# A long-convolution and routed low-rank FFN kernel: the tables' last steps behind the gates, row sums and gate transposes on the Vector engine

## The chip, the cores and the metric

The kernel runs on one core of a Trainium2 chip. The metric is the time of one execution in device microseconds (us); lower is better. The core has five engines that each work through their own instructions in order: TensorE (PE, matrix products), VectorE (DVE), ScalarE (ACT), GpSimd (POOL) and SyncE (SP). DMA transfers are started from the queues of SP, ACT and POOL. [...]

## The reference

The input x has shape (64 batches, 64 heads, 1024 positions). For every head h a convolution kernel K of length 1024 is made from 64 complex modes, and each row is convolved with it and masked by a length per batch. The result goes through a layer of 64 low-rank experts, of which each token uses 16, and x is added.

```
dtA = A * dt[:, None]                                  # 64 heads x 64 modes, complex
Cs  = Cc * (exp(dtA) - 1) / A
K   = 2 * real(einsum('hn,hnl->hl', Cs, exp(dtA[:, :, None] * arange(1024))))
y   = causal_conv(x * mask, K) + x * mask * D[:, None]; y = y * mask

scores = y @ Wr.T                                      # 4096 tokens x 64 experts
top_vals, top_idx = top_k(scores, 16); gates = softmax(top_vals)
G   = zeros.at[token, top_idx].set(gates)
h   = einsum('nd,krd->nkr', y, A)                      # 64 experts of rank 16: 1024 columns
out = einsum('nkr,kdr->nd', h * G[:, :, None], B)
return x + 2 * out
```

## The kernel before, in words

The 4096 tokens are 64 heads times 64 batches. They are worked through in eight groups g of eight heads, 512 tokens each. A group has these stages:

- **Tables** (`tables(g)`, lines 237 to 347, a generator whose yields let other work come in between). Vector and Scalar make the powers of the modes: f, k and a clamp on Vector, Sin and Exp on Scalar, and from them w (real and imaginary part, 129 positions). From w come the tiles b (`L320` on Scalar, `L366` on Vector), which PE transposes against the identity (pb, `L326`); Scalar copies them to bt (`L330`). The first 128 values of K of each head are the sums of b over the modes. PE takes these sums as a product with a tile of ones (pk, `L293`, a result of 2 partitions by 512); Scalar copies it to ks, Vector adds D to the first column, and SP writes the rows to memory (krows) and reads them back as Toeplitz tiles (toep).
- **Convolution** (`conv(g)`, line 595). PE forms the states of seven blocks (pu, `L620`), Scalar copies them to s, and Vector runs a recurrence over the blocks (`recur`, `L366`, three instructions per block and pair of heads; four pairs a group). PE adds the part inside a block (pc from x and toep, `L649`) and that of earlier blocks (pc from s and w, `L658`), and Vector applies the mask and writes y (`L666`).
- **Gates** (`gates(g)`, line 722). PE computes scores (psh, `L728`, eight products into two halves of a bank), Scalar copies them to sh, and PE transposes sh (psc, `L737`) so that tokens lie on partitions. Vector adds the two halves (sc), takes the 16 largest by two rounds of max and match_replace, and with Scalar's Exp forms the softmax in the tile sa.
- **Spreading the gates** (`spread_gates`, line 768). PE transposes sa back (pg, `L772`), Scalar copies pg to gt, and a DMA on Scalar's queue writes gt to memory. Eight DMAs (on GpSimd's queue, for the last group on SP's) read it back as gx, each gate repeated for the 16 ranks of its expert.
- **First product** (`first`, line 795). h = y times A, by a seven-product scheme on quarters (`seven`, `L553`, products 1, 6, 2, 7, 5, 4, 3 for each of two column blocks j). Vector and GpSimd combine the products (u, p), multiply them by the gates gx into the tile hg, and form sums of hg; GpSimd's queue stores hg to memory.

While a group's convolution is computed, the products of the group before fill PE. After all groups, a second stage (`second`, from about 630 us on) computes h times B in two levels of the same scheme.

The order of instructions on each engine comes from a scheduler that works at build time from the order of the program and the dependences; some rows are pinned with `tc.keep_in_program_order`. Buffers count: the PSUM pool ps_k (two banks) serves pb, pk, pu, psh, psc and pg; ps_f (four banks) serves h; the tables' tiles mag, f, k and sn are single, and k and sn are reused as the tiles b. The tile gt is reused for sh.

The last yields of `tables(g)` are taken here, at the end of `conv` of the group before:

```
last_two = inside(2), inside(3)
across(*last_two[0])
across(*last_two[1])
step(6)                       # the last steps of the next group's tables
```

The main loop then calls `gates(g, y)`, runs what is left of the tables' steps, starts the products of the group, and calls `spread_gates`.

Of the kernel before, what the change touches and what calls it, by code (L numbers as in the profile page):

```python
# [37 lines left out]
F32 = mybir.dt.float32  # L38
I32 = mybir.dt.int32
AF = mybir.ActivationFunctionType  # L40
ALU = mybir.AluOpType
AX = mybir.AxisListType
PSUM = bass.MemoryType.PSUM

P = 128
# [5 lines left out]
NE = 64  # L51
# [3 lines left out]
HG = 8  # L55
NG = NH // HG
TOK = HG * NB
NTT = TOK // P
# [5 lines left out]
GP = HG // 2  # L64
NW = P + 1
NCH = NBLK - 1
KROW = P - 1 + P
# [22 lines left out]
    return c  # L90


def body(ctx: ExitStack, tc, x, xo, lens, par, dvec, at, bm, wt, cst, out):
    nc = tc.nc
    V = nc.vector
    G = nc.gpsimd
# [11 lines left out]
    ps_k = psum.enter_context(tc.tile_pool(name="ps_k", bufs=2, space=PSUM))  # L108
# [4 lines left out]
    gp = pool(left, "gp", 1, "left")  # L113
    tq = pool(left, "tq", 1, "left")
    ids = pool(ctx, "ids", 1, "right")
    const = pool(right, "const", 1, "right")
    xp = pool(right, "xp", 4, "right")
    tp = pool(right, "tp", 1, "right")
    tabp = pool(right, "tabp", 1, "right")
# [8 lines left out]
    cst_sb = ids.tile([P, NW + P + 2 + NBLK], F32, tag="cst", name="cst_sb")  # L128
    nc.scalar.dma_start(cst_sb, cst)
    lens_sb = prep.tile([P, NB], I32, tag="lens", name="lens_sb")  # L130
    d_sb = const.tile([2, NP], F32, tag="dvec", name="d_sb")
    nc.scalar.dma_start(d_sb, dvec)
    lv = cst_sb[:, :NW]
    ident = cst_sb[:, NW : NW + P]
    heads = cst_sb[:, NW + P : NW + P + 2]
# [2 lines left out]
    krows = dram.tile([NH, KROW], F32, tag="krows", name="krows")  # L138
# [98 lines left out]
    def tables(g):  # L237

        j0 = g * GP
        wide = [P, GP, NW]

        def new(t, name=None):
            return tabp.tile(wide, F32, tag=t, name=f"{name or t}_{g}")

        mag, f, k = new("mag"), new("f"), new("k")
        for i in range(GP):
            nc.scalar.activation(mag[:, i, :], lv, AF.Exp, scale=dt_re[:, j0 + i : j0 + i + 1])
        tt(f, tu_hi[:, j0 : j0 + GP].unsqueeze(2).to_broadcast(wide),  # L250
           lv.unsqueeze(1).to_broadcast(wide), ALU.mult)
        yield
        ts(k, f, MAGIC, ALU.add, MAGIC, ALU.subtract)
        yield
        tt(f, f, k, ALU.subtract)
        yield
        for i in range(GP):
            stt(f[:, i, :], lv, tu_lo[:, j0 + i : j0 + i + 1], ALU.mult, f[:, i, :], ALU.add)
            if i % 2:
                yield  # L260
        ts(f, f, HALF_IN, ALU.min, -HALF_IN, ALU.max)

        sh, sn = new("k", "sh"), new("sn")
        nc.scalar.activation(sh, f, AF.Sin, scale=math.pi)
        nc.scalar.activation(sn, f, AF.Sin, scale=2.0 * math.pi)
        nc.scalar.activation(sh, sh, AF.Square)
        nc.scalar.activation(sh, sh, AF.Copy, scale=-2.0, bias=1.0)
        yield
        w = tab2.tile([P, 2, GP, NW], F32, tag="w", name=f"w_{g}")
        tt(w[:, 1], mag, sn, ALU.mult)  # L270
        yield
        tt(w[:, 0], mag, sh, ALU.mult)
        yield
        alpha, nbeta, nalpha = (scales[q] for q in ("alpha", "nbeta", "nalpha"))
        bt = tp.tile([P, GP, 2 * P], F32, tag="bt", name=f"bt_{g}")

        def others():
            return (tab2.tile([P, 3, GP], F32, tag="turn", name=f"turn_{g}"),
                    tp.tile([P, HG, P], F32, tag="toep", name=f"toep_{g}"))

        if g == 0:
            turn, toep = others()
            tabs[g] = (w, bt, turn, toep)
        h0 = g * HG
        all_rows = tabp.tile([2, GP, P], F32, tag="ks", name=f"ks_{g}")

        def kernels(bbs, i):


            n = i + 2 * len(bbs)  # L290
            pk = ps_k.tile([2, n - i, P], F32, tag="pk", name=f"pk_{g}_{i}")
            for m, bb in enumerate(bbs):
                nc.tensor.matmul(pk[:, 2 * m : 2 * m + 2, :], lhsT=heads, rhs=bb[:, :, 0, :],  # L293
                                 start=True, stop=True)
            ks = all_rows[:, i:n, :]
            nc.scalar.copy(ks, pk)
            return ks, i, n

        def rows(ks, i, n):

            tt(ks[:, :, 0], ks[:, :, 0], d_sb[:, j0 + i : j0 + n], ALU.add)
            row = krows[h0 + 2 * i : h0 + 2 * i + 1, :]
            nc.sync.dma_start(
                krows[h0 + 2 * i : h0 + 2 * n, P - 1 :].rearrange("(i a) l -> a i l", a=2), ks)
            nc.sync.dma_start(toep[:, 2 * i : 2 * n, :],
                              bass.AP(row.tensor, row.offset, [[1, P], [KROW, 2 * (n - i)], [1, P]]))

        bbs, halves = [], []
        for i in range(GP):
            j = j0 + i  # L310
            re, im = w[:, 0, i, :P], w[:, 1, i, :P]
            if i % 2 == 0:
                bb = tabp.tile([P, 2, 2, P], F32, tag=("sn", "k")[i // 2], name=f"b_{g}_{i}")
                bbs.append(bb)
            b = bb[:, i % 2]
            for c, by in enumerate((alpha, nbeta)):
                if g == 0:
                    ts(b[:, c, :], re, by[:, j : j + 1], ALU.mult)
                else:
                    nc.scalar.activation(b[:, c, :], re, AF.Copy, scale=by[:, j : j + 1])  # L320
            stt(b[:, 0, :], im, nbeta[:, j : j + 1], ALU.mult, b[:, 0, :], ALU.add)
            stt(b[:, 1, :], im, nalpha[:, j : j + 1], ALU.mult, b[:, 1, :], ALU.add)
            if g == 0 or i % 2 == 0:
                pb = ps_k.tile([P, 1 if g == 0 else 2, 2 * P], F32, tag="pk", name=f"pb_{g}_{i}")
            for c in range(2):
                nc.tensor.transpose(pb[:, i % 2 if g else 0, (1 - c) * P : (2 - c) * P], b[:, c, :], ident)  # L326
            if g == 0:
                nc.scalar.copy(bt[:, i, :], pb[:, 0])
            elif i % 2:
                nc.scalar.copy(bt[:, i - 1 : i + 1, :], pb)  # L330
            if g == 0 and i % 2:
                halves.append(kernels(bbs[i // 2 :], i - 1))
            if g == 0 and i == 3:
                rows(*halves[0])
            yield
        if g:
            turn, toep = others()
        V.tensor_copy(turn[:, 0:2], w[:, :, :, P])
        ts(turn[:, 2], turn[:, 1], -1.0, ALU.mult)
        if g == 0:  # L340
            yield
            rows(*halves[1])
            return
        ks = kernels(bbs, 0)
        yield
        rows(*ks)
        tabs[g] = (w, bt, turn, toep)


# [4 lines left out]
    def tt(o, a, b, o_):  # L354
        V.tensor_tensor(out=o, in0=a, in1=b, op=o_)  # L355
        return o
# [54 lines left out]
    s, q = parts  # L411
# [183 lines left out]
    def conv(g, steps, out):  # L595
        if g == 0:
            next(steps)
        w, bt, turn, toep = tabs.pop(g)
# [74 lines left out]
        def step(n):  # L673
            for _ in range(n):
                next(steps, None)
# [40 lines left out]
        last_two = inside(2), inside(3)  # L716
        across(*last_two[0])
        across(*last_two[1])
        step(6)


    def gates(g, y):
        yf = y.rearrange("p k s h b -> p k (s h b)")

        phalf = ps_k.tile([P, TOK], F32, tag="pk", name=f"psh_{g}")
# [4 lines left out]
                start=(d < 2), stop=(d >= NBLK - 2),  # L730
            )
        sh = gp.tile([P, TOK], F32, tag="gt", name=f"sh_{g}")
        nc.scalar.copy(sh, phalf)

        pscore = ps_k.tile([P, NTT, 2, NE], F32, tag="pk", name=f"psc_{g}")
        for t in range(NTT):
# [13 lines left out]
        for t in range(NTT):  # L750
# [3 lines left out]
        ex = sa  # L754
# [8 lines left out]
            out=ex, in0=ex, in1=rd.unsqueeze(2).to_broadcast([P, NTT, NE]), op=ALU.mult)  # L763
        return ex

    gt_dram = dram.tile([NG, NE, TOK], F32, tag="gt", name="gt_dram")

    def spread_gates(g, ex, spread):

        pg = ps_k.tile([NE, TOK], F32, tag="pk", name=f"pg_{g}")  # L770
        for t in range(NTT):
            tc.keep_in_program_order(nc.tensor.transpose(pg[:, t * P : (t + 1) * P], ex[:, t, :], ident))  # L772
        gt = gp.tile([NE, TOK], F32, tag="gt", name=f"gt_{g}")
        nc.scalar.copy(gt, pg)
        nc.scalar.dma_start(gt_dram[g], gt)
        n = P // RANK
        queue = nc.sync if g + 1 == NG else G
        for j in range(0, KH, 2):
            for m in range(2):
                gx = gxp.tile([P, 2, TOK], F32, tag="gx", name=f"gx_{g}_{j}_{m}")  # L780
                for ii in range(2):
                    c = m * KH + j + ii
                    i = queue.dma_start(  # L783
                        gx[:, ii, :],
                        gt_dram[g, c * n : (c + 1) * n, :].unsqueeze(1).to_broadcast([n, RANK, TOK]),
                    )
                    if queue is nc.sync:
                        tc.keep_in_program_order(i)
                spread[m, j] = gx
# [315 lines left out]
    def steps_of(g):  # L1105
        return tables(g) if g < NG else iter(())
# [21 lines left out]
    for g in range(NG):  # L1128
        ex = gates(g, y)
# [17 lines left out]
        if g == 0:  # L1147
            tables1, n = steps_of(1), 0
# [50 lines left out]
    n = 0  # L1199
    for _ in products:  # L1200
# [3 lines left out]
        if n in (5, 6):  # L1204
            i = (1, 6)[n - 5]
# [77 lines left out]
```

## Time and profile before

| what | value |
|---|---|
| median of 3 runs | 975.63 us (975.53 to 976.57) |
| the profiled execution | 975.34 us |
| its span in the profile | 973.6 us |
| granted TensorE clock | 1.0 |
| Vector, reduction of psc (sc), 8 times | 0.689 us each |
| Vector, reduction den over 256 elements, 8 times | 0.412 us each |
| Scalar, copy of gt from pg, 8 times | 0.579 us each |
| Scalar, copy of ks from pk (2 by 512), 7 times | about 0.58 us each |
| ACT_TABLE_LOAD on Scalar | 1.283 us each, 17 times |

The span is what the profiler saw from the first to the last instruction; the time of the execution is 1.7 us longer. A row of a timeline gives the start in us from the span's begin, the length, the engine, the line of the program, the operation, what it writes and reads, the shape, and the number of instructions of that kind that follow each other. Square brackets name idle time of the engine just before, and what ended it. A product in float32 appears as two instructions. The mean length of a product in the groups overlaps with that of the next one, since matmuls are pipelined; the distance of starts is what one costs. Names leave out buffer numbers: h is the first product's bank, s in the first stage the state tiles, ty the sums of y, gx the spread gates.

### The profile page before, as it was taken

The page shows a single profiled execution, that of the slowest core. Times are in us where ns is not written, and L with a number is a line of the kernel's source. Part 1 is how long each engine was busy: PE and PEld are TensorE (multiplying, and loading weights), DVE is VectorE, ACT ScalarE, POOL GpSimd, SP SyncE. Part 2 cuts the span into 40 slices and gives each one's busy share as a digit, 9 for nine tenths or more (in the row PEclk, how much of TensorE's full clock was granted, in tenths as well). Part 3 has the DMA queues.
Part 4 walks back from the last instruction along what each step waited for, and adds up shares of the span by engine and source line. Part 5 has one row for each costly group of instructions (what it writes and reads, how often), then busy time and mean ns, then how long its engine had stood idle before and what let it go on. Part 6 is the DMA issues. An engine that isn't in the chain of part 4 may idle for free.

```text
span 973.6 us, 11950 instructions
## 1 busy us (share of the span) xinstructions
PE 961.4 (99%) x4312; PEld 726.0 (75%) x4312; DVE 725.6 (75%) x1682; ACT 160.2 (16%) x310; POOL 330.5 (34%) x285
## 2 busy tenths in 40 slices
PE   7999999999999999999999999999999999999998
PEld 2476666676676686686676678888888888888887
DVE  8889887497597597686656769778966775686674
ACT  5344051230230230131101000000000000000000
POOL 0212212041023023022122122247545563854565
PEclk9999999999999999999999999999999999999999
DMA  7825334234325315315415254682674467267432
GB/s 281 228 52 171 101 105 141 92 107 137 109 79 164 109 38 167 126 55 157 140 31 159 77 181 163 206 299 97 216 264 132 166 198 250 83 216 269 132 109 108
DMA packets 67456, 143.99 MB, mean 148 GB/s; under 512 B 9478, under 2 KB 18246, under 8 KB 67398
## 3 DMA queue, kind: packets, MB, share of 16 engines
q1 hardware_dynamic: 49378, 94.40, 28.8%
q0 software_dynamic: 16864, 47.22, 15.3%
q10 hardware_dynamic: 1156, 1.61, 0.7%
q8 instruction: 34, 0.56, 0.2%
q14 instruction: 24, 0.20, 0.1%
HBM read 94.89 MB, written 47.25 MB: 146 GB/s over the span
## 4 chain that ended last, share of the span: by engine, by line
PE 95%; DVE 4%; issue 0%; DMA 0%; ACT 0%; DVEq 0%
PE h L553 39%; PE s L1048 34%; PE pc L649 6%; PE pc L658 5%; PE pu L620 5%; PE psh L728 3%; PE pb L326 1%; PE pk L293 1%; DVE y L666 1%; PE pg L772 0%; PE last L1048 0%; DVE ty L355 0%; PE psc L737 0%; DVE f L355 0%; DMA par_sb<-in_par 0%
## 5 line engine op out<-in xcount | busy, mean ns | idle before, releaser
L366 DVE SCALAR_TENSOR_TENSOR s<-s,turn 128x128 f32<-128x128 f32 (+1 forms) x558 | 151.1, 320 | 25.6 <-ACT s L625 20.2
L553 PE MATMUL h<-y,waa 128*128 128x256 f32 x512 | 120.7, 383 | 0.0
L553 PE MATMUL h<-y,was 128*128 128x256 f32 x512 | 117.4, 381 | 0.0
L553 PE MATMUL h<-ty,was 128*128 128x256 f32 x512 | 116.3, 379 | 0.0
L553 PEld LDWEIGHTS h<-y,waa 128*128 128x128 f32 x512 | 94.7, 190 | 26.6 <-issue 14.4
L553 PEld LDWEIGHTS h<-y,was 128*128 128x128 f32 x512 | 96.1, 190 | 20.0 <-issue 6.4
L553 PEld LDWEIGHTS h<-ty,was 128*128 128x128 f32 x512 | 97.0, 190 | 14.5 <-issue 1.5
L810 POOL TENSOR_TENSOR hg<-h_p,gx 128x512 f32<-128x512 f32 x16 | 27.1, 1694 | 217.9 <-DVE h_p L366 140.6
L810 POOL TENSOR_TENSOR hg<-h_u,gx 128x512 f32<-128x512 f32 x32 | 46.8, 1465 | 112.3 <-DVE h_u L355 112.2
L666 DVE TENSOR_TENSOR y<-pc,mask 128x512 f32<-128x512 f32 x64 | 41.2, 683 | 47.9 <-PE pc L658 47.9
L1062 ACT COPY p<-s 128x512 f32<-128x512 f32 x28 | 16.4, 586 | 312.4 <-PE s L1048 312.4
L907 POOL TENSOR_TENSOR o<-o,acc_a 128x512 f32<-128x512 f32 x32 | 47.6, 1506 | 41.4 <-ACT acc_a L925 21.7
L649 PE MATMUL pc<-x,toep 128*128 128x512 f32 x128 | 58.9, 593 | 0.1
L553 PE MATMUL h<-ty,waa 128*128 128x256 f32 x256 | 58.6, 381 | 0.0
L625 ACT COPY s<-pu 128x448 f32<-128x448 f32 x62 | 32.7, 532 | 146.1 <-PE pu L620 145.7
L553 PEld LDWEIGHTS h<-ty,waa 128*128 128x128 f32 x256 | 48.1, 190 | 9.9 <-issue 3.5
L783 POOL DMA_DIRECT2D gx<-gt_dram x56 | 33.5, 629 | 63.9 <-DMA gt_dram<-gt 63.9
L620 PE MATMUL pu<-x,bt 128*64 128x448 f32 x256 | 53.5, 549 | 0.0
L658 PE MATMUL pc<-s,w 64*128 64x448 f32 x248 | 52.8, 555 | 0.0
L907 POOL TENSOR_TENSOR o<-o,b_room 128x512 f32<-128x512 f32 x32 | 49.1, 1556 | 9.8 <-DVE b_room L355 9.8
L355 DVE TENSOR_TENSOR o<-o,s 128x512 f32<-128x512 f32 x50 | 34.0, 681 | 23.0 <-PE s L1048 17.9
L813 POOL DMA_DIRECT2D hg_dram<-hg x32 | 25.6, 801 | 69.4 <-DVE hg L355 45.5
(236 smaller groups left out, 1607.1 us busy)
## 6 DMA issues: line engine op xcount, KB each, us to landing
x<-in_x SPq DMA_DIRECT2D x32, 512.0 KB
hg_dram<-hg POOLq DMA_DIRECT2D x16, 1024.0 KB, 5.2
o<-in_xo SPq DMA_DIRECT2D x64, 256.0 KB
out<-o SPq DMA_DIRECT2D x63, 256.0 KB
gx<-gt_dram POOLq DMA_DIRECT2D x56, 256.0 KB, 6.3
qy<-hg_dram SPq DMA_DIRECT2D x28, 512.0 KB
r<-hg_dram SPq DMA_DIRECT2D x26, 512.0 KB
hg_dram<-hg POOLq DMA_DIRECT2D x16, 768.0 KB, 4.4
```

The source lines that it names most:

```text
L355: V.tensor_tensor(out=o, in0=a, in1=b, op=o_)
L366: V.scalar_tensor_tensor(out=o, in0=a, scalar=s, in1=b, op0=o1, op1=o2)
L553: nc.tensor.matmul(bank[:, ii, :], lhsT=fac[n - 1][:, k, (j + ii) * P : (j + ii + 1) * P], rhs=rf[n - 1][:, k, :], start=(first and ii == ...
L620: nc.tensor.matmul(pu[hh * NS : (hh + 1) * NS, :], lhsT=bt[:, i, (1 - c) * P + hh * NS : (1 - c) * P + (hh + 1) * NS], rhs=xt[:, hh, : NCH ...
L625: marks["s"] = nc.scalar.copy(s[:, c], pu.rearrange("p (k b) -> p k b", b=NB))
L649: nc.tensor.matmul(pc, lhsT=toep[:, 2 * i + hh, :], rhs=xt[:, hh, :], start=True, stop=False)
L658: m = nc.tensor.matmul(pcs[hh][:, NB:], lhsT=w[o : o + NS, c, i, 1:], rhs=s[o : o + NS, c].rearrange("p k b -> p (k b)"), start=False, sto ...
L666: marks["y"] = V.tensor_tensor(out=y[:, :, i // 2, 2 * (i % 2) + hh, :], in0=pcs[hh].rearrange("p (k b) -> p k b", b=NB), in1=mask, op=ALU ...
L783: i = queue.dma_start(gx[:, ii, :], gt_dram[g, c * n : (c + 1) * n, :].unsqueeze(1).to_broadcast([n, RANK, TOK]),)
L810: G.tensor_tensor(out=o, in0=a, in1=b, op=op)
L907: tc.keep_in_program_order(G.tensor_tensor(out=o, in0=a, in1=b, op=op_))
L1048: nc.tensor.matmul(bank[:, ii, :], lhsT=left_[i - 1][:, k, ii * P : (ii + 1) * P], rhs=right_[i - 1][:, k, :], start=(first and ii == rows ...
```

## The change

Four things change in the groups; the second stage stays.

1. The row sums of the tables of groups 1 to 7 are taken by Vector: one reduction over bt gives kc (128 positions by 8 heads), PE transposes kc to 8 by 128, Scalar copies it, Vector adds D with one value per head (a new small input, dgrp), and SP writes eight rows of 512 bytes.
2. `step(6)` at the end of `conv` is dropped, so the last six steps of the next tables stand behind `gates(g)` in the program.
3. The gates are transposed by one Vector instruction in blocks of 32 by 32 instead of four PE transposes and a Scalar copy, and leave in two DMAs.
4. Tokens are numbered anew in the gates: the copy from psh to sh reads every fourth column, so that token 4p + t lies on partition p of transpose t. With that order the block transposes leave 128 consecutive tokens of an expert in one partition, and each DMA writes runs of 128 values (512 bytes).

The tile of ks in group 0 now shares the buffer of mag.

```
-        all_rows = tabp.tile([2, GP, P], F32, tag="ks", name=f"ks_{g}")
+        if g == 0:
+            all_rows = tabp.tile([2, GP, P], F32, tag="mag", name=f"ks_{g}")
...
+        def kernels_by_vector():
+            kc = tabp.tile([P, HG], F32, tag="kc", name=f"kc_{g}")
+            V.tensor_reduce(kc.rearrange("p (i a) -> p i a", a=2),
+                            bt[:, :, P:].rearrange("p i (a n) -> p i a n", a=2), AX.X, ALU.add)
+            pk = ps_k.tile([HG, P], F32, tag="pk", name=f"pk_{g}")
+            nc.tensor.transpose(pk, kc, ident)
+            ks = tabp.tile([HG, P], F32, tag="ks8", name=f"ks8_{g}")
+            nc.scalar.copy(ks, pk)
+            return ks
+
+        def rows_by_head(ks):
+            tt(ks[:, 0:1], ks[:, 0:1], d_of_group[:, g : g + 1], ALU.add)
+            row = krows[h0 : h0 + 1, :]
+            nc.sync.dma_start(krows[h0 : h0 + HG, P - 1 :], ks)
+            nc.sync.dma_start(toep, bass.AP(row.tensor, row.offset, [[1, P], [KROW, HG], [1, P]]))
...
-        ks = kernels(bbs, 0)
+        ks = kernels_by_vector()
         yield
-        rows(*ks)
+        rows_by_head(ks)
...
         across(*last_two[1])
-        step(6)
...
-        nc.scalar.copy(sh, phalf)
+        nc.scalar.copy(sh.rearrange("e (t p) -> e t p", t=NTT), phalf.rearrange("e (p t) -> e t p", t=NTT))
...
-        pg = ps_k.tile([NE, TOK], F32, tag="pk", name=f"pg_{g}")
-        for t in range(NTT):
-            tc.keep_in_program_order(nc.tensor.transpose(pg[:, t * P : (t + 1) * P], ex[:, t, :], ident))
-        gt = gp.tile([NE, TOK], F32, tag="gt", name=f"gt_{g}")
-        nc.scalar.copy(gt, pg)
-        nc.scalar.dma_start(gt_dram[g], gt)
+        q = 32
+        gt = gp.tile([P, NE // q, P], F32, tag="gt", name=f"gt_{g}")
+        V.transpose(gt.rearrange("p b (j t) -> p t b j", t=NTT), ex.rearrange("p t (b i) -> p t b i", i=q))
+        for b in range(NE // q):
+            nc.scalar.dma_start(
+                gt_dram[g, b * q : (b + 1) * q, :].rearrange("i (a k) -> a i k", k=P), gt[:, b, :])
```

One more load, `nc.scalar.dma_start(d_of_group, dgrp)` (8 by 8 values), stands at the start on Scalar's queue.

More of the change, by code (lines that the diff above doesn't have):

```diff
@@ L90, in constants, with body @@
     return c
-def body(ctx: ExitStack, tc, x, xo, lens, par, dvec, at, bm, wt, cst, out):
+def body(ctx: ExitStack, tc, x, xo, lens, par, dvec, dgrp, at, bm, wt, cst, out):
     nc = tc.nc
@@ L132, in body @@
     nc.scalar.dma_start(d_sb, dvec)
+    d_of_group = const.tile([HG, NG], F32, tag="dgrp", name="d_of_group")
+    nc.scalar.dma_start(d_of_group, dgrp)
     lv = cst_sb[:, :NW]
@@ L1261 @@
         "dvec": D.reshape(NP, 2).T,
+        "dgrp": D.reshape(NG, HG).T,
         "at": A.reshape(NE * RANK, NBLK, P).transpose(2, 1, 0),
```

## Prediction

> **What bounds the kernel now.** I read the page's busy line and the chain that ended last, then the timeline of TensorE (PE) at a group boundary, then Vector's (DVE) at the same place. The page and the chain:
>
> ```profile
> PE 961.4 (99%) x4312; PEld 726.0 (75%) x4312; DVE 725.6 (75%) x1682; ACT 160.2 (16%) x310; POOL 330.5 (34%) x285
> PE 95%; DVE 4%; issue 0%; DMA 0%; ACT 0%; DVEq 0%
> ```
>
> PE is busy 99%, and 95% of the chain is PE. One rule of the Trainium skill speaks against resting on the first figure: "Trainium Kernel Development and Optimization", section Performance Expectations, says that matmul busy time is a bad measure because matmuls are pipelined, and that weight-load time tells more. By that rule the row to read is 75%, PE need not be the bound, and taking PE work away brings nothing (975.6 us). So I look at starts. PE at the boundary of group 3 (start, length, instructions):
>
> ```profile
> 331.49 0.70 PE L553 MATMUL h<-y,waa 128*128 128x256 f32 x2
> 332.34 1.26 PE L326 MATMUL pb<-cst_sb,b 128*128 128x128 f32 x8
> 333.43 0.60 PE L553 MATMUL h<-y,waa 128*128 128x256 f32 x2
> 333.96 1.02 PE L293 MATMUL pk<-b,cst_sb 128*2 128x256 f32 x4
> 334.92 3.65 PE L728 MATMUL psh<-y,wt_sb 128*64 128x512 f32 x16
> 338.50 1.99 PE L553 MATMUL h<-y,waa 128*128 128x256 f32 x8
> 340.33 0.60 PE L737 MATMUL psc<-cst_sb,sh 128*128 128x128 f32 x4
> 341.63 3.62 PE L553 MATMUL h<-y,was 128*128 128x256 f32 x16
> 345.09 3.62 PE L553 MATMUL h<-ty,was 128*128 128x256 f32 x16
> ...
> 362.35 0.60 PE L772 MATMUL pg<-cst_sb,sa 128*64 128x128 f32 x4
> 362.88 3.23 PE L620 MATMUL pu<-x,bt 128*64 128x448 f32 x16
> ```
>
> Sixteen h start every 3.46 us (341.63 to 345.09), one each 0.216 us, although a mean in the groups is 0.38: the array is fed without gaps. I therefore follow the starts, not the rule, and price PE work from start to start, never by means. Next the busy time of one stretch behind the boundary (bounds, length, then busy us and instructions of PE, weight loads, Vector, Scalar, GpSimd; granted clock, DMA share, GB/s), and two rows at the use of a recurrence:
>
> ```profile
> 345.00:365.20 20.20, 20.20 (x100) 16.36 (x100) 18.56 (x33) 7.55 (x18) 7.29 (x5) 1.00 0.13 47
> ...
> 297.37 0.68 DVE L355 TENSOR_TENSOR h_u<-h,h_u 128x512 f32<-128x512 f32 x1
> 302.21 1.02 PE L658 MATMUL pc<-s,w 64*128 64x448 f32 x4
> ```
>
> PE has no gap there, and Vector is 92% busy (18.56 of 20.20). In the second pair the recurrence s of two pairs has ended at 297.37, and PE first uses it at 302.21: 4.8 us of room. Vector is thus the engine that comes next.
>
> **The change, part by part.** Seven groups build a table behind group 0, and eight spread gates.
>
> *Row sums leave PE.* pk, four matmul halves, takes 333.96 to 334.92, 0.96 us; the same at the other boundaries, and 0.95 in group 0. Seven of them: 6.7 us off PE. In their place stands one 128x128 transpose of kc per group; four transposes take 0.43 to 0.53 (psc, pg), one with its change of shape I take as 0.15: 1.05 us back. Net 5.65.
>
> *Gate transposes leave PE.* pg takes 362.35 to 362.88, 0.53 us, in six groups, and 0.44 in the first and last: 4.06. In group 1 PE also waits 0.5 us for pg's input; that goes: 4.56 in all. A second rule speaks against this edit: "VectorE: DVE Perf Modes", section Rules for kernel authors, would keep a 128x128 transpose on TensorE where PSUM will do as its target. By it these 4.56 us stay and the whole change brings about 0.5. With PE full and Vector idle at the boundary I go by the rows.
>
> *Psh moves ahead of the tables' transposes.* The built order at groups 1 to 6 becomes: two rows of h (4 halves), psh, two rows of h, psc, pb (4), one row of h, pb (4), three rows of h, two rows of the next product, pk. Group 7, which has no table, already runs so:
>
> ```profile
> 559.94 1.29 DVE L666 TENSOR_TENSOR y<-pc,mask 128x512 f32<-128x512 f32 x2 [0.22 <-PE pc L658]
> 561.28 3.65 PE L728 MATMUL psh<-y,wt_sb 128*64 128x512 f32 x16 [0.31 <-DVE y L666]
> 565.84 0.60 PE L737 MATMUL psc<-cst_sb,sh 128*128 128x128 f32 x4
> 566.47 0.69 DVE L739 TENSOR_REDUCE sc<-psc 128x256 f32<-128x512 f32 x1 [5.24 <-PE psc L737]
> 569.77 0.68 DVE L817 TENSOR_TENSOR hg<-h,gx 128x512 f32<-128x512 f32 x1
> ```
>
> So psh waits 0.31 for the last y; six times, 1.9. What goes is pb's wait for y's bank, about 0.15 each (PE is idle from 332.19 to 332.34): 0.9 back. Net loss 1.0.
>
> *A new wait at pk.* kc stands on Vector behind top-k's last match_replace. Measured from psh's start: Vector passes that point at 569.77 - 561.28 = 8.49; kc reads 512 elements, as sc's reduction does (0.69), so it ends at 9.18 and PE may load it at 9.24. PE reaches pk after psh 3.59, h 0.97, psc 0.43, pb 0.50, h 0.43, pb 0.54, h 1.30 and h 0.86: 8.62. It waits 0.62, six times: 3.7 us. Behind pk stands all of PE. The price of kc is bounded by den's 0.41 (256 elements) and by 1.7, sc stretched by the 1.07 that Vector loses beside a GpSimd product (ty takes 2.28 instead of 1.21); GpSimd is idle there (0 us of 331 to 349), so I take 0.69. In group 0 kc is early and pk waits for nothing.
>
> *Vector's load.* Added: seven kc and eight 32-by-32 transposes. No row shows such a transpose: below, 0.35 (256 elements at den's rate without its start); above, 2.3 (as long as the stretched ty); I take den's 0.41, as it reads the same 256 elements, and more than 10 us lie between it and the next pu in most groups. The larger thing is order: k, f, the four f, the clamp and w, about 3.6 us, ran between y and sc, where Vector otherwise waits up to 5.24 us; they now stand behind the gates, since k's buffer comes free only at the later pb. With hg (0.6, behind ks now), kc and the transpose Vector has 4.7 us more after match_replace, but gets there 3.6 us earlier (345.00 less 332.94 + 8.49) and had 1.6 idle before s. Its recurrence in groups 3 to 6 begins at about the same absolute time, some 0.5 us later against PE, of the 4.8 of room. In group 2 the product in flight is one later, pu comes 3.5 us sooner, and the room is nearly used: I add 0.4 us once.
>
> *Scalar, DMA, GpSimd.* The gt copy (0.58) goes; sh is read from PSUM with a step of four: no row shows such a read, at best 0.59, at worst twice that, when psc would start 0.5 later, 3 us in all; 0.59 taken, as Scalar's copies follow the number of elements alone (448: 0.53, 512: 0.59). Scalar waits at the gates' store for Vector's transpose, by my count 11 us in group 2 and 4 in later ones; behind it stand the Sin table load, Sin, and the next p copy, which PE needs only after pu (3 us of room in group 2; if it is late, PE waits by as much). gt goes out as two DMAs of 512-byte runs (0.45 each to issue) instead of one; on GpSimd the gx issues (0.6 each) now stand between the products and before the last hg store, which moves about 1 us and has some 9 us until hg is written again (beyond that, Vector's next gate product would wait for the store). gx is asked for 10 us earlier: I cost that at nothing, since x loads are issued between 302 and 329 and not there; had they met, a gx load (6.3 us to landing) would still have some 10 us. SP's krows and toep follow pk, 7 us later, with 30 us until pc (8 in group 0, where they are not later). The extra dgrp load on Scalar's queue costs 0.5 us before a table load that waits for cst until 3.44 anyway (0.5 if it did not).
>
> Sum: 5.65 + 4.56 - 1.0 - 3.7 - 0.4 = 5.1 us less. The profiled execution took 975.34 (span 973.6), so 970.2; the runs' median, 975.63, lies 0.3 above it: **970.5**.
>
> **Rivals.**
> A, the sum above: 970.5, with 969 to 973 for the sizes.
> B, *pk's wait doesn't happen* (kc at den's price or PE later than I count): 3.7 back, 966.8. Against it: the 8.49 is measured.
> C, *Vector becomes the bound, slower than before.* If the added 4.7 us grow by 5 (transpose at 2.3, three moved operations stretched by 1.07 beside GpSimd, as ty is), the recurrence overruns its room by some 0.7 us in groups 3 to 6, by 4 to 5 in group 2 and 2 in group 1: 9.3 us of PE waits at pc<-s, against 5.1 won: 979.8. It decides once s begins more than about 7 us behind the first pu (2.3 us now). For it: Vector's 92%; against: 19 us of idle Vector in each group of 73 (53.7 busy from 272 to 345).
> D, *half of C, or a slow strided read*: the gain is eaten, 974 to 976.5.
> That the change leaves PE work where it was is excluded by the built order: pg and the old pk are gone.
>
> **How the numbers follow.** A 0.62, B 0.14, D 0.10, C 0.14. Faster is under 973.7, slower over 977.6 (0.2%, about what a measurement here can tell from no change): 0.76, 0.10, 0.14. The range leaves out C and the far end of B: 966.4 to 975.8.
>
> **What would show it.** Right: PE busy some 9 us lower, pg gone, a wait of about 0.6 us at pk for kc six times, psh waiting for y 0.3 each, pc<-s waiting for nothing. Wrong: pc<-s waiting for Vector's s by whole microseconds (C), psc waiting for Scalar's sh (D), no wait at pk (B).

## The result and the profile after

The changed kernel takes 968.99 us (median of 6 runs, 968.88 to 969.07) against 975.58 us for the kernel before on the same chip (975.39 to 976.57): 6.6 us less, ratio 0.9928 with a 95% interval of 0.9914 to 0.9941. The forecast was 970.5, so 1.5 us too high, with the sign and the mechanism right. The profiled execution took 968.97 us with a span of 967.2; before it was 975.34 with 973.6, so spans and medians tell the same difference.

The page of the changed kernel, its busy line and its chain of work that ended last:

```profile
PE 952.2 (98%) x4259; PEld 721.4 (75%) x4259; DVE 732.1 (76%) x1697; ACT 152.1 (16%) x302; POOL 335.2 (35%) x285
PE 94%; DVE 5%; issue 0%; DMA 0%; ACT 0%; DVEq 0%
```

TensorE (PE) is busy 9.2 us less (961.4 before), Vector (DVE) 6.5 us more. The span fell by only 6.4: some of what TensorE was spared has come back as waiting. The busy share cannot show that; the timeline of TensorE at the boundary that the prediction showed does. (The prediction calls it the boundary of group 3; counted from 0, as the program counts, its psh is that of group 4.) Each row has the start, the length, the number of instructions, and in brackets the idle time in front and who ended it:

```profile
327.62 1.13 PE L575 MATMUL h<-y,waa 128*128 128x256 f32 x4
329.06 3.65 PE L749 MATMUL psh<-y,wt_sb 128*64 128x512 f32 x16 [0.31 <-DVE y L688]
332.65 1.13 PE L575 MATMUL h<-y,waa 128*128 128x256 f32 x4
333.61 0.60 PE L759 MATMUL psc<-cst_sb,sh 128*128 128x128 f32 x4
334.05 0.60 PE L348 MATMUL pb<-cst_sb,b 128*128 128x128 f32 x4
...
335.49 1.46 PE L575 MATMUL h<-y,waa 128*128 128x256 f32 x6
336.79 1.03 PE L575 MATMUL h<-y,was 128*128 128x256 f32 x4
338.28 0.27 PE L309 MATMUL pk<-cst_sb,kc 128*8 128x128 f32 x1 [0.47 <-DVE kc L306]
338.39 2.76 PE L575 MATMUL h<-y,was 128*128 128x256 f32 x12
...
354.80 3.62 PE L575 MATMUL h<-ty,was 128*128 128x256 f32 x16
358.34 3.23 PE L642 MATMUL pu<-x,bt 128*64 128x448 f32 x16
```

The old pk of 0.96 us is now one transpose that costs 0.11 from start to start (338.28 to 338.39), and no pg stands in front of pu. New are the two waits in brackets. Vector at the same place shows why pk is late and what the new transpose costs, and two groups of instructions give the means over the whole run (busy us, then mean ns of one):

```profile
337.55 0.68 DVE L306 TENSOR_REDUCE kc<-bt 128x8 f32<-128x512 f32 x1
342.89 0.63 DVE L796 STREAM_TRANSPOSE gt<-sa 128x256 f32<-128x256 f32 x1
...
L796 DVE STREAM_TRANSPOSE gt<-sa 128x256 f32<-128x256 f32 x8 | 5.1, 641 | 0.1
L755 ACT COPY sh<-psh 128x512 f32<-128x512 f32 x8 | 4.7, 586 | 122.3 <-PE psh L749 122.3
```

kc starts 8.49 us after psh (337.55 - 329.06), to the hundredth the figure of the prediction, and pk follows at 9.22 (9.24 counted). The strided read of psh by Scalar takes 0.586, as a plain one did. TensorE's waits in the groups (us in total, times, longest):

```profile
PE pk L309 <- DVE kc L306: 2.8, 6, 0.5
PE psh L749 <- DVE y L688: 2.2, 7, 0.3
```

No pc waits for Vector's states, as rival C would have had it. Behind the gates of group 2, where the prediction saw the least room, Vector is through with them and begins the h_u behind them 2.6 us before TensorE's first use:

```profile
220.30 0.68 DVE L377 TENSOR_TENSOR h_u<-h,h_u 128x512 f32<-128x512 f32 x1
...
222.90 1.77 PE L680 MATMUL pc<-s,w 64*128 64x448 f32 x8
```

The gain by stretch, read from the first pu behind each boundary, before less after: 0.9 us at the first, 2.5 at the second, 3.2 at the third (210.68 and 207.46), then about 0.66 more at each (3.9, 4.5, 5.2, 5.9), and 6.35 where the second stage begins. Nothing changes behind that.

### The profile page after: what moved, and what is told of

Same layout as the page of the kernel before. It is cut to its first block, busy times and chain, and to the rows that moved or that the text cites. A ratio compares the mean times of both kernels' runs of the same rounds, so it can differ in the third digit from the quotient of the medians.

```text
span 967.2 us, 11861 instructions
## 1 busy us (share of the span) xinstructions
PE 952.2 (98%) x4259; PEld 721.4 (75%) x4259; DVE 732.1 (76%) x1697; ACT 152.1 (16%) x302; POOL 335.2 (35%) x285
## 4 chain that ended last, share of the span: by engine, by line
PE 94%; DVE 5%; issue 0%; DMA 0%; ACT 0%; DVEq 0%
PE h L575 38%; PE s L1072 34%; PE pc L671 6%; PE pc L680 5%; PE pu L642 5%; PE psh L749 3%; DVE y L688 1%; DVE sa L769 0%; DVE sb L773 0%; DVE sc L761 0%; DVE kc L306 0%; DVE m L767 0%; PE psc L759 0%; PE last L1072 0%; DVE m L771 0%
## 5 line engine op out<-in xcount | busy, mean ns | idle before, releaser
L834 POOL TENSOR_TENSOR hg<-h_p,gx 128x512 f32<-128x512 f32 x16 | 30.1, 1883 | 249.6 <-DVE h_p L388 219.1
L807 POOL DMA_DIRECT2D gx<-gt_dram x56 | 34.0, 624 | 43.1 <-DMA gt_dram<-gt 43.1
L931 POOL TENSOR_TENSOR o<-o,u 128x512 f32<-128x512 f32 x36 | 45.3, 1280 | 10.0 <-DVE u L377 9.7
```

Of the source, the lines that this page charges most:

```text
L807: i = queue.dma_start(gx[:, ii, :], gt_dram[g, c * n : (c + 1) * n, :].unsqueeze(1).to_broadcast([n, RANK, TOK]),)
L834: G.tensor_tensor(out=o, in0=a, in1=b, op=op)
L931: tc.keep_in_program_order(G.tensor_tensor(out=o, in0=a, in1=b, op=op_))
```

## The experiments

The theory (P) is the prediction's: the time follows what TensorE does and waits for, from start to start; Vector has room. Times in one table, all medians; the ratio is to the kernel before, run beside each. The sections below say what each row tells apart.

| kernel | us | ratio, 95% interval |
|---|---|---|
| the change | 968.99 | 0.9928 (0.9914 to 0.9941) |
| gates' half alone | 971.58 | 0.9953 (0.9936 to 0.9971) |
| row sums' half alone, step dropped | 977.44 | 1.0013 (1.0002 to 1.0024) |
| row sums' half alone, step kept | 969.62 | 0.9940 (0.9926 to 0.9953) |
| dropped step alone | 977.13 | 1.0011 (1.0002 to 1.0021) |
| the change, step kept | 965.41 | 0.9891 (0.9871 to 0.9911) |
| the change, pk later | 965.67 | 0.9901 (0.9887 to 0.9914) |
| the change, tokens not renumbered | 969.11 | 0.9937 (0.9925 to 0.9949) |
| the change, 4 / 12 / 24 more transposes in each group | 968.70 / 970.44 / 977.26 | 0.9931 / 0.9948 / 1.0016 |

### The gates' half alone

The kernel before with the strided copy of psh and the spread by Vector put in:

```diff
-        nc.scalar.copy(sh, phalf)
+        nc.scalar.copy(sh.rearrange("e (t p) -> e t p", t=NTT), phalf.rearrange("e (p t) -> e t p", t=NTT))
...
-        pg = ps_k.tile([NE, TOK], F32, tag="pk", name=f"pg_{g}")
...
+        V.transpose(gt.rearrange("p b (j t) -> p t b j", t=NTT), ex.rearrange("p t (b i) -> p t b i", i=q))
```

> Only the gates' half of the change: Vector transposes them, the tokens are renumbered, the row sums stay on TensorE. Theory P (the time follows TensorE's own work and waits): pg goes, 6 x 0.53 + 2 x 0.44 = 4.1 us, and nothing comes in its place, 975.6 - 4.1 = 971.5 (971.0 to 972.0). Rival V (Vector is at its limit): the 8 transposes of 0.64 us show again, 976 or more. Rival D (the long runs to memory matter in themselves): more than 4.5 us less.

Measured: 971.58, against 975.5 before: 3.9 less, for 4.1 expected. In the steady groups the pu come every 75.66 us (360.34, 436.00) instead of every 76.10 (362.88, 438.98): 0.44 a boundary. Of the 0.53 of pg, 0.09 come back, since sixteen h in front of pu now take 3.55 from start to start (356.79 to 360.34) where they take 3.46 elsewhere. Nothing is charged for the transposes of 0.64 us on Vector. V and D fall.

### The row sums' half alone, and the dropped step alone

The first is the changed kernel with the gates as before (the diff above, reversed). The second is the kernel before with one line less:

```diff
         across(*last_two[1])
-        step(6)
```

> Only the row sums' half: summed by Vector behind the top-k, transposed by TensorE, the step in front of the gates left out as in the change; gates as before. Theory P: 7 x 0.96 of the old pk go, 7 x 0.11 of the new come, and the wait of 0.63 at pk six times, 6.7 - 0.8 - 3.8 = 2.1 us less: 973.5 (973.0 to 974.0). Rival O (the wait at pk stands where TensorE would have waited anyway): the full 5.9 less, 969.7.

> The kernel before, with only the last call of the tables' steps in front of the gates left out, so that the tables' transposes and row sums by TensorE stand behind the gates. Theory P as read from the trace after: the wait of psh for y and the saved changes of shape cancel, no difference, 975.6 (975.0 to 976.2). The prediction's own term: 1.0 us more, 976.6. Rival O (the order alone makes the gain): 2 to 6 us less.

Theory P failed in both: 977.44 and 977.13, slower than before by 1.9 and 1.6 us, where it had 2.1 less and no difference. (The prediction's own term for the swap, 1.0, gave 976.6 for the dropped step, 0.5 from the measured.) What the count had left out is a wait that neither before nor after shows. From the waits of the dropped step alone, and from the timelines of TensorE and Scalar with the row sums alone, behind the gates of group 2:

```profile
PE pu L620 <- ACT gt L773: 0.4, 2, 0.3
```

```profile
208.45 0.60 PE L796 MATMUL pg<-cst_sb,sa 128*64 128x128 f32 x4
208.98 0.97 PE L642 MATMUL pu<-x,bt 128*64 128x448 f32 x4
212.55 4.13 PE L642 MATMUL pu<-x,bt 128*64 128x448 f32 x12 [2.60 <-ACT gt L798]
216.61 3.72 PE L575 MATMUL h<-y,waa 128*128 128x256 f32 x16
...
210.75 0.40 ACT L342 ACTIVATE b<-w,p_alpha 128x128 f32<-128x128 f32 x1 [1.65 <-DVE w L377]
...
211.64 0.39 ACT L342 ACTIVATE b<-w,p_nbeta 128x128 f32<-128x128 f32 x1
211.94 0.56 ACT L798 COPY gt<-pg 64x512 f32<-64x512 f32 x1
```

pg and the pu that follow it share a pool of two banks in the code (`ps_k`). The second pu needs pg's bank, which is free only when Scalar has copied gt out of it; and Scalar's queue holds that copy behind four b of the next tables, which wait for Vector's w. TensorE spends 7.63 us from 208.98 to 216.61 on a row of pu that takes 3.16 elsewhere (210.68 to 213.84 before): 4.5 us at one place.

The bank is not all of it. Three stretches of the same trace, with the columns that the prediction named (the granted clock is the third figure from the end):

```profile
208.98:213.20 4.22, 1.62 (x9) 0.54 (x10) 4.09 (x11) 2.35 (x8) 0.79 (x1) 1.00 0.64 244
213.25:216.60 3.35, 3.35 (x10) 0.73 (x6) 1.34 (x5) 1.67 (x4) 1.55 (x3) 0.50 0.25 55
216.70:222.00 5.30, 5.30 (x25) 4.68 (x26) 4.72 (x23) 3.69 (x8) 3.13 (x6) 1.00 0.99 254
```

Shortly after the wait the clock granted to TensorE is halved for some 3.4 us. The twelve pu behind the wait take 4.06 us (212.55 to 216.61), where twelve of sixteen take 2.37 (three quarters of 3.16). So 1.7 of the 4.5 us are the clock, and 2.8 the bank. The 14 executions agree: ten have a mean clock of 0.998, as the profiled one has, and a median of 977.5; three of the four at 1.000 took 975.5 to 975.8, as long as the kernel before, and one 977.5. Only one execution was profiled, so that the wait brings the clock down is not shown by an experiment; that even without the drop the half gives nothing is shown by those three.

In the kernel before, the last of these b had started at 200.76, and the copy followed pg at once, at 210.78; with the step dropped, the tables' work stands behind the gates, and w and b come as late as the copy. The dropped step alone shows the small form of the same: its pu come every 76.66 us or more in the three groups where the row of pu is interrupted or stretched for gt, and after 76.29 where it isn't (440.43 to 516.72), against 76.10 before. So the order costs 0.19 a boundary by itself and about 0.4 more where the bank is held.

This is why the halves don't add up. The gates' half gives 3.9; the row sums' half with the dropped step loses 1.9; together they give 6.6, not 2.0. The difference, 4.6, is about what that one place costs. The gates' half removes pg, and with it the copy that TensorE had to wait for.

### The step kept: with both halves, and with the row sums alone

The opposite of the dropped step: the line `step(6)` is put back in the changed kernel, so that the tables' transposes, Vector's row sums and pk come in front of psh and the top-k. Once with the gates by Vector, once with the gates by TensorE.

> The changed kernel with the step in front of the gates kept: tables' transposes, Vector's row sums and pk stand before psh and before the top-k. Theory P: kc then waits for the last y and one sum of 1.2 us instead of the top-k, TensorE has 6 products of h (0.49 each) and 8 pb (0.11) to run meanwhile, some 3.9 us against 3.5 us that kc needs, so the wait of 0.63 goes six times and nothing else changes: 969.0 - 3.8 = 965.2 (964.5 to 966.5). Rival W (kc comes later than that in front of the gates, and psh and the top-k queue behind pk): 970 or more. Rival O (the dropped step makes the gain): 971 or more.

> Only the row sums' half, with the step in front of the gates kept and gates by TensorE as before. Theory P (the loss of the row sums' half alone came from its order: the wait at pk, that of psh, and states that wait for a bank that the gates hold): all three go, 7 x 0.96 - 7 x 0.11 = 5.9 us less than before, 969.6 (969.0 to 970.5). Rival V (Vector's sums in themselves delay the gates that TensorE then waits for): 972 or more.

Measured: 965.41 and 969.62, each within 0.3 us of theory P. TensorE's wait for y at psh, with both halves, and the same boundary as above, with Vector's kc:

```profile
PE psh L750 <- DVE y L688: 0.3, 1, 0.3
```

```profile
325.99 0.70 PE L575 MATMUL h<-y,waa 128*128 128x256 f32 x2
326.84 1.25 PE L348 MATMUL pb<-cst_sb,b 128*128 128x128 f32 x8
327.93 2.32 PE L575 MATMUL h<-y,waa 128*128 128x256 f32 x10
330.09 0.27 PE L309 MATMUL pk<-cst_sb,kc 128*8 128x128 f32 x1
330.29 3.65 PE L750 MATMUL psh<-y,wt_sb 128*64 128x512 f32 x16
...
329.21 0.68 DVE L306 TENSOR_REDUCE kc<-bt 128x8 f32<-128x512 f32 x1
```

kc is done at 329.89 and pk starts at 330.09: the bracket at pk is gone, and the one at psh too, except in group 7, which has no tables. The pu come every 74.82 us (281.28, 356.10) instead of every 75.44 in the changed kernel (282.90, 358.34): 0.62, the price of the wait at pk. With the step kept the halves do add up: 3.9 and 5.7 (975.32 - 969.62) make 9.6, and together they give 10.1 (975.5 - 965.41). This version beats both kernels, the changed one by 3.6 us.

### pk later

The wait could also be taken away from the other side. Vector's order stays that of the change; on TensorE pk is issued later. In five of the six groups where it waited, sixteen instructions of the next product stand in front of it instead of four:

```diff
             pk = ps_k.tile([HG, P], F32, tag="pk", name=f"pk_{g}")
-            nc.tensor.transpose(pk, kc, ident)
+            if g > 1:
+                with tc.issue_after(marks["mm"][-3].ins):
+                    nc.tensor.transpose(pk, kc, ident)
...
-            for _ in steps:
-                pass
+            for v in steps:
+                if v == "kc":
+                    ahead(products, 2)
```

Here `marks["mm"]` lists the products of h, and the tables' steps yield "kc" between the sum and its transpose.

> The changed kernel with pk issued three products of h (3 x 0.49 us) later on TensorE in five of the six groups where it waited, and Vector's work as it was. Theory P (the wait at pk is TensorE's loss, 0.63 each, and nothing close behind needs the row sums): 5 x 0.63 = 3.1 us less than the change, 965.8 (965.3 to 966.5). Rival T (the tables' transfers behind pk are what is late, and come 1.5 us later still): 969 or more.

Measured: 965.67, 3.3 less than the change. TensorE's waits:

```profile
PE psh L756 <- DVE y L695: 2.2, 7, 0.3
PE pk L312 <- DVE kc L306: 0.5, 1, 0.5
```

One wait at pk is left, at the first of the six (129.14), where the trace has pk behind four instructions of h as before. No wait of TensorE for anything made from the row sums appears. That the wait at pk is TensorE's own loss, some 0.63 each, is thus shown in two ways. The seven waits of psh stand here and the time is within 0.3 us of the version that has none but one, so the swap of psh and pb costs next to nothing in the changed kernel.

### Vector's room

More transposes behind each real one, into a tile that is dead by then:

```diff
+        for _ in range(4):
+            V.transpose(marks["sb"], ex)
```

> The changed kernel with four more transposes of the gates on Vector behind each real one (into a dead tile, 8 x 4 x some 0.55 us = 17.6 us of Vector in all, 2.2 us in each group). Theory P (Vector has room: 2.6 us in front of the states in group 2, over 4 in the later ones): no more than 0.5 us, 969.0 to 969.5. Rival V (Vector is at or near its limit): the 2.2 us show in each of the groups 1 to 6, 980 or more.

> As the run with four more transposes in each group, with twelve: they measured 0.43 us each there, so 5.1 us of Vector in each group. Theory P: in group 2 the recurrence ended 3.4 us ahead of its use with four in place (219.1 against 222.5), and eight more are 3.4 us: at the edge, 968.7 to 972. Rival V as the prediction has it (room of 4.8 us in the later groups, and every group behind that shows): 970 to 973 with waits of pc for s in several groups.

> The same with twenty-four, 10.3 us of Vector in each group. Theory P: 5.1 us beyond twelve, which are at the edge, so some 4 to 5 us in each of the groups 1 to 6: 993 to 1003. If it stays under 980, Vector has far more room than the trace shows.

Measured: 968.70, 970.44 and 977.26. Four cost nothing. Twelve cost 1.5 us, nearly all of it in the convolution of group 1 (73.96 from its first pu to psh at 121.57, where the change has 73.81 and 120.01), most of that where pk fell between the pu (that row takes 4.26 instead of 3.20); later the pu come every 75.44 us as before, and no pc waits for s, as rival V would have had it. Twenty-four, 10.4 us of Vector in each group, cost 8.3 us and not 24 or more: the last expectation was far off. With twenty-four, the added transposes, TensorE's waits in the groups, its timeline at the longest one and the clock behind that:

```profile
L799 DVE STREAM_TRANSPOSE sb<-sa 128x256 f32<-128x256 f32 x192 | 83.2, 433 | 0.9
...
PE h L575 <- DVE h_p L388: 3.1, 1, 3.1
PE pk L309 <- DVE kc L306: 2.8, 6, 0.5
PE psh L749 <- DVE y L688: 2.3, 7, 0.4
PE pc L680 <- DVE s L388: 2.1, 4, 0.8
...
603.18 5.41 PE L575 MATMUL h<-y,was 128*128 128x256 f32 x16 [3.13 <-DVE h_p L388]
608.42 3.62 PE L575 MATMUL h<-y,waa 128*128 128x256 f32 x16
...
603.85:607.10 3.25, 3.25 (x10) 2.54 (x9) 3.25 (x4) 0.00 (x0) 2.02 (x2) 0.50 0.00 0
```

Now, at last, pc waits for s, the mark of rival C, but by 2.1 us in all. By the last group's second row of pu TensorE is 3.3 us behind the change (538.34 against 535.08). One wait of 3.1 comes in the products of group 7, and behind it the clock is 0.50 again: that row of h takes 5.24 us instead of 3.46, 1.8 more. Of the 14 executions, the six with a mean clock of 1.000 have a median of 976.0, the other eight lie at 977.2 to 979.2; so about 7 of the 8.3 us are the added work. The room at the recurrence was not a fixed 4.8 us. The built order places Vector's instructions anew when there are more of them, and work with a late due time (h_u, hg, the b of the next tables, even some of the added transposes) goes behind or between the recurrence's steps. So a count that adds all new work in front of the recurrence takes too much.

### Tokens not renumbered

The changed kernel with a plain copy of psh, the transpose's blocks written in the tokens' own order, and gates stored in runs of 128 bytes instead of 512:

```diff
-        V.transpose(gt.rearrange("p b (j t) -> p t b j", t=NTT), ex.rearrange("p t (b i) -> p t b i", i=q))
+        V.transpose(gt.rearrange("p b (t j) -> p t b j", t=NTT), ex.rearrange("p t (b i) -> p t b i", i=q))
```

> The changed kernel without the renumbering of the tokens: psh is copied in order, and each row of gates goes to memory in 16 runs of 128 bytes instead of 4 of 512. Theory P (the gates' transfer lies beside TensorE's work with time to spare): no difference, 968.5 to 969.5. Rival D (the short runs make the gates late for the products of the last group, which stores them at once): 1 us more or over, 970 or more.

Measured: 969.11, no difference that can be told from 968.99. The long runs are worth nothing here, and the transpose itself is cheaper without them:

```profile
L796 DVE STREAM_TRANSPOSE gt<-sa 128x256 f32<-128x256 f32 x8 | 3.5, 436 | 0.1
```

0.436 us against 0.641 for the same 128x256 numbers: the renumbering's output, where neighbours of one block lie four numbers apart, costs Vector 0.2 us each. GpSimd's wait for the stored gates is 47.7 us in all against 43.1; TensorE waits for GpSimd in neither. (The profiled execution took 970.54: TensorE waited 1.7 us for toep in group 0, before there were any gates.)

## Why the prediction came out right, and where its terms were off

**The bound.** Starts of TensorE, not its mean durations, carried the sum, and the runs agree: removing work from TensorE that is in the chain gave its start-to-start price each time (gates 3.9 for 4.06 counted from pg alone, row sums with the step kept 5.7 for 5.9 in its expectation). The rule weighed first ("Trainium Kernel Development and Optimization", Performance Expectations), taken as the prediction took it, would have left 975.6; the measurement decides against that use of it here. The page speaks of how close a kernel is to its roofline, not of which engine holds the chain. The rule weighed second ("VectorE: DVE Perf Modes", Rules for kernel authors) would have kept the gates' transposes on TensorE; the run of the gates' half alone puts 3.9 us on Vector's side, in a kernel where TensorE is full and Vector is not. That rule speaks of a whole 128x128 transpose; the change needs blocks of 32 by 32 only, since the DMAs put the blocks in their places, so it applied less than the prediction allowed.

**Row sums, 5.65.** Right: 0.96 goes, and the new pk costs 0.11 and not 0.15, which makes it 5.95.

**Gates, 4.56.** Too much by 0.7: the half alone gave 3.9, although the wait of 0.5 in group 1 went too. What was left out is the 0.09 that comes back at a steady boundary, and that the first boundary gave only 0.09 of 0.44 (the next pu at 74.66 instead of 74.75).

**The wait at pk, 3.7.** Right in place, cause and size: six times, 0.62 counted. The waits view gives 0.47 each, but the starts lose 0.63 (0.62 by the run with the step kept): pk reaches the array at 338.28, while the h in front of it, left to run on, would have let it start at 337.65 (336.79 + 0.86).

**Psh ahead of the tables' transposes, 1.0.** Mis-sized. The wait of psh for y came as counted, 0.31 seven times. But one boundary less its pk takes 9.17 us (327.62 to 336.79) against 9.18 before (331.49 to 341.63, less 0.96): what the wait costs, the other side gives back, pb's wait and the joins between pb and h. In the kernel before, the same swap costs 0.19 a boundary, some 1.1 in all, near the term; it did not carry over.

**Group 2's room, 0.4.** Not used: 2.6 us were left there. It was the wrong kind of term as well, since Vector's order adapts.

**Vector's load.** The transpose was taken at 0.41 and takes 0.641; kc was taken at 0.69 and takes 0.676. Eight times 0.23 is 1.9 us of Vector, and none of it shows, as four further transposes in each group show nothing either. Rival C, 14% in the forecast, looks too likely in hindsight: its 5 us of extra Vector work in each group is what the run with twelve transposes had, and that took 970.44, not 979.8.

The sum with these terms as measured (0.3 more for pk, 1.0 and 0.4 not charged, 0.7 less for the gates) is 6.1 less, against 6.6 measured; 0.5 is not assigned. At a steady boundary nothing is left over: 0.85 for pk and 0.44 for pg, less 0.63 for the wait, make the 0.66 by which the pu come sooner. Since the gates' term erred to the other side than the rest, part of the nearness of 970.5 is luck.

**What the prediction did not see.** It priced the dropped step at the wait of pk and the swap, and the sum came out; but with the row sums on Vector the dropped step is also what costs 4.5 us behind the gates of group 2 as long as pg is there (2.8 for the bank, 1.7 for the clock). And it did not ask whether the order itself was worth having. The version with the step kept shows that it was not: the change gives up 3.6 of the 10.1 us that its two halves bring.

## What to carry to other kernels

Where one engine is full, price an edit by that engine's starts, then price the order that comes with it apart from the work: here the work was worth 10.1 us and the new order cost 3.6, nearly all of it at a transpose of 0.11 us that stood behind a top-k on another engine. When a result moves off the full engine, either make its input early or let the full engine run other work until it comes; both cured the same wait. And test the halves of a change in pairs: a half that gains nothing alone can be worth 2.6 us with the other (968.99 against 971.58), because the other removes the copy that TensorE would wait for.

## What the hardware showed that I had not expected

- A transpose in 32 by 32 blocks of 128x256 float32 on Vector takes 0.436 us into rows written in order and 0.641 into rows where a block's neighbours lie four numbers apart. I had taken one figure, 0.41, without asking how the output is laid out.
- Scalar's read of psh at a step of four numbers takes 0.586 us, the same as in order. On Vector's side the step of four is in what it writes, on Scalar's in what it reads, so the two do not compare the engines.
- The idle time that the profile puts in front of a matmul, 0.47 us at pk, is less than what the starts lose there, 0.63.
- Behind a wait of 2.6 us in one trace and of 3.1 us in another, TensorE's granted clock was 0.50 for some 3.4 us; the work in that time took 1.7 and 1.8 us more. The wait costs more than its own length there.
